# Mean and variance as sums on ScalarE, inputs rounded a pair of tiles ahead, and another order of the opening, in a block with fp4-rounded feed-forward layers

## The chip, the cores and the metric

The kernel runs on one core of one Trainium2 chip. The metric is the time of one execution on the device in microseconds (us); lower is better. Engines are named as the profile names them: PE is TensorE's matmul queue and PEld its weight loads, DVE is VectorE, ACT is ScalarE, POOL is GpSimd and SP is SyncE, which issues most transfers.

## The reference

The input x holds 2 x 2048 rows of D = 256 float32 numbers. Three parts follow each other, each with a layer norm in front and added back to x:

```python
x = x + 0.5 * ffn(layernorm(x))
x = x + attention(layernorm(x))
x = x + 0.5 * ffn(layernorm(x))

def layernorm(x):                       # over the 256 numbers of a row
    return (x - mean(x)) / sqrt(var(x) + 1e-5)

def fp4_quant_dequant(x):               # blocks of 16 along the last dimension
    scale = max(max(abs(block)) / 6, 1e-12)
    return round_to_grid(block / scale) * scale      # grid 0, .5, 1, 1.5, 2, 3, 4, 6, with sign

def fp4_linear(x, w):
    return fp4_quant_dequant(x) @ fp4_quant_dequant(w).T

def ffn(x):                             # w_gate, w_up: 704 x 256, w_down: 256 x 704
    return fp4_linear(silu(fp4_linear(x, w_gate)) * fp4_linear(x, w_up), w_down)
```

The attention has complex projections of 512 numbers from 256, a softmax over 2048 keys, and an output projection back to 256. Biases are added to all of its projections.

## The kernel before

**Tiles.** The 4096 rows make 32 tiles of 128 rows. Eight tiles share one SBUF array, xs[g], with g from 0 to 3. Everything stays in SBUF and all arithmetic is float32.

**Norm (L186 to L225).** One Norm object measures n tiles of a group. DVE does a bn_stats of each tile (L201), a bn_aggr of each (L204) and adds EPS (L206). ACT takes the square root (L209), which needs another function table than Silu (L442) or the exponential (L744); the switch is a row ACT_TABLE_LOAD. DVE refines the reciprocal with one Newton step (L212 to L221) and forms shift = -mean * rstd (L224). An Identity activation on ACT with both as pointers (L234) then writes the normalised tile.

**Rounding.** quant (L158 to L184) and the class Rounding (from L247 on, used in the opening) round to fp4: a reduction over blocks of 16 for the scale (L164), scale and reciprocal (L166, L168), a multiply (L170), an Abs on ACT (L179), two steps on DVE (L180, L182), and a last multiply by the scale (L184). For inputs and for pairs of h the last multiply runs on POOL.

**Feed-forward part.** inputs(i0) takes four tiles: the norm of the group if i0 is at its beginning, L234, the rounding of the 128 x 1024 array xl, and the transposes tx on PE (L403), whose results ACT copies to xqT (L404). products(i) computes gate and up of a tile on PE into gu (L428; PSUM has two buffers), with Silu on ACT (L442) and the multiply h = silu(gate) * up on DVE (L446). Two tiles of h are rounded together. turn(i) transposes h (th, L463) and copies it out on ACT (hqT, L464). back(i) multiplies by w_down (po, L472) and adds to x on DVE (L474). Tiles go through as units of two. At the first unit of every four tiles the whole of inputs for the next four is issued, ahead of the unit's products.

**Opening.** Up to about 90 us the weights are folded, rounded and transposed while tiles 0 to 11 are normalised and rounded and tiles 0 to 7 go through their products. These jobs are generators ("threads"), and the string ORDER names which one issues its next step: n0, n1 and n2 are norms of tiles 0 to 3, 4 to 7 and 8 to 15; g, u and d are halves of the weights; f folds the attention weights; x0 to x5 are inputs, two tiles each; p0 to p7 are products; h0 to h3 round pairs of h; t and b are turn and back. A fence ties every instruction to the one before it on its engine, so that the written order is the engines' order.

**Behind the opening** a scheduler orders each engine's instructions. Tiles 8 to 31 of the first feed-forward part run to about 300 us, the attention to about 840 us (scores ps at L708, the exponential at L744, products m at L805), and the second feed-forward part to the end. The norms of the attention and of the second feed-forward part are called early (measure in class Batch, and inputs), so that their instructions lie between others.

Of the kernel before, what the change touches and what calls it, by code (L numbers as in the profile page):

```python
# [10 lines left out]
FP = mybir.dt.float32  # L11
I32 = mybir.dt.int32
AF = mybir.ActivationFunctionType
ALU = mybir.AluOpType
# [3 lines left out]
P = 128  # L18
BLK = 16
EPS = 1e-5  # L20

# [4 lines left out]
BELOW = 1.0 - 2.0**-22  # L28
# [1 line left out]


ORDER = """
n0 n0 n0 g0 g0 g0 g0 n0 n0 g0 n0 g1 n0 g1 n0 f n0 g1 g0 n0 f g0 f n0 f g1 n0 g0 g1 x1 u1 x0 x1 u0 x0
f g1 f u0 g0 u1 g1 f x0 x1 g1 u0 x0 f n1 u1 g1 f f n1 u0 x0 n1 x0 x1 f n1 n1 u1 x1 n1 d1 u0 u1 x1 u0
n2 g1 n1 n2 n1 f u1 x0 d1 g1 n1 x0 x1 x0 n1 f u1 g0 x0 n1 x1 g0 p0 n1 x3 u1 u0 x2 p1 u1 n2 p0 d0 u1
x3 x1 u0 u0 x3 d0 d1 n2 d0 d1 d1 u1 p1 n2 x2 n2 u0 n2 x3 u0 x2 d0 x3 x1 n2 x3 x2 n2 p0 x3 x2 n2 d1
x2 d0 n2 p0 d0 n2 x3 n2 p1 p3 x2 p1 n2 x2 f n2 d0 h0 p3 d1 d0 h0 n2 p2 d1 p2 h0 x3 x4 x3 p3 x4 h0 x4
p3 p2 x2 p2 x4 x5 x5 h1 d0 x2 x5 p6 p4 x4 h0 h0 p6 p5 h1 x4 h0 p4 d1 x4 h0 x4 h1 p5 p4 p5 h1 h0 h1
x5 p4 d0 p5 p7 x4 h1 h2 d1 t0 p7 d1 x5 h1 x5 h2 t0 h1 p6 x5 p6 h2 h2 t1 p7 h1 h2 p7 h3 x4 d0 t1 x5
h2 b0 h3 t2 h3 x5 h3 t2 h2 b1 b0 t3 x5 h2 t3 h3 b1 h3 h3 b2 h2 h3 b3 b2 b3 h3  # L40
"""
TURNED = 4

# [9 lines left out]
def kernel(ctx: ExitStack, tc: tile.TileContext, x, wqT, bq, wkT, bk, wvT, bv, woT, bo,  # L53
                        w_gate, w_up, w_down, out):
    nc = tc.nc
    NB, S, D = x.shape
# [3 lines left out]
    GT = 8  # L60
# [76 lines left out]
    make_identity(nc, ident)  # L137
    ones = const.tile([P, P], FP, tag="ones", name="ones")
    nc.gpsimd.memset(ones, 1.0)
    tiny = const.tile([P, 1], FP, tag="tiny", name="tiny")  # L140
    nc.gpsimd.memset(tiny, 1e-12)

    wgu = const.tile([P, KD, 2 * FF], FP, tag="wgu", name="wgu")
    wd = const.tile([P, NR, D], FP, tag="wd", name="wd")
    nc.gpsimd.memset(wd[0:P - LAST, NR - 1, :], 0.0)
# [8 lines left out]
    def all_of(parts):  # L154
        for _ in parts:
            pass

    def quant(pool, y, n, tag, last, first=None):  # L158


        nb = n // BLK
        yb = y.rearrange("p (b k) -> p b k", k=BLK)
        scale = pool.tile([P, nb], FP, tag=f"{tag}_s", name=f"{tag}_s", bufs=2)
        nc.vector.tensor_reduce(scale, yb, AX.X, ALU.max, apply_absolute_value=True)  # L164
        yield
        nc.vector.scalar_tensor_tensor(scale, scale, 1.0 / 6.0, tiny.to_broadcast([P, nb]), ALU.mult, ALU.max)  # L166
        rec = pool.tile([P, nb], FP, tag=f"{tag}_r", name=f"{tag}_r", bufs=2)
        nc.vector.reciprocal(rec, scale)  # L168
        if first is None:
            nc.vector.scalar_tensor_tensor(  # L170
                yb, yb, BELOW, rec.unsqueeze(2).to_broadcast([P, nb, BLK]), ALU.mult, ALU.mult
            )
        else:
            nc.vector.scalar_tensor_tensor(rec, rec, BELOW, ones[:, 0:nb], ALU.mult, ALU.mult)
            first.tensor_tensor(yb, yb, rec.unsqueeze(2).to_broadcast([P, nb, BLK]), ALU.mult)
        yield

        m = pool.tile([P, n], FP, tag=f"{tag}_m", name=f"{tag}_m", bufs=2 if pool is wpool else 1)
        nc.scalar.activation(m, y, AF.Abs, scale=STEPS)  # L179
        nc.vector.scalar_tensor_tensor(y, m, LEAST, y, ALU.max, ALU.add)  # L180
        yield
        nc.vector.scalar_tensor_tensor(y, m, LEAST, y, ALU.max, ALU.subtract, reverse1=True)  # L182
        yield
        last.tensor_tensor(yb, yb, scale.unsqueeze(2).to_broadcast([P, nb, BLK]), ALU.mult)  # L184

    class Norm:  # L186

        def __init__(self, g, j0, n):  # L190
            self.g, self.j0, self.n = g, j0, n

        def turns(self, pool):
            g, j0, n = self.g, self.j0, self.n

            def tile(what, shape):
                return pool.tile(shape, FP, tag=what, name=f"{what}{g}_{j0}")

            mv, bn = tile("mv", [P, n, 2]), tile("bn", [P, n, 6])
            for j in range(n):  # L200
                nc.vector.bn_stats(bn[:, j, :], xs[g][:, j0 + j, :])  # L201
                yield
            for j in range(n):
                nc.vector.bn_aggr(mv[:, j, :], bn[:, j, :])  # L204
            var = tile("var", [P, n])
            nc.vector.tensor_scalar(var, mv[:, :, 1], EPS, None, ALU.add)  # L206
            yield
            sd = tile("sd", [P, n])
            nc.scalar.activation(sd, var, AF.Sqrt)  # L209
            yield  # L210
            self.rstd = rstd = tile("rstd", [P, n])
            nc.vector.reciprocal(rstd, sd)  # L212
            yield

            nc.vector.tensor_tensor(sd, rstd, rstd, ALU.mult)
            yield
            nc.vector.tensor_tensor(sd, sd, var, ALU.mult)
            yield
            nc.vector.tensor_scalar(sd, sd, -0.5, 1.5, ALU.mult, ALU.add)
            yield  # L220
            nc.vector.tensor_tensor(rstd, rstd, sd, ALU.mult)  # L221
            yield
            self.shift = tile("shift", [P, n])
            nc.vector.scalar_tensor_tensor(self.shift, mv[:, :, 0], -1.0, rstd, ALU.mult, ALU.mult)  # L224
            yield  # L225

    def normalise(pool, g, j0, n):
# [19 lines left out]
    class Rounding:  # L247
# [6 lines left out]
        def tile(self, what, n, bufs):  # L254
            return self.pool.tile([P, n], FP, tag=f"{self.tag}_{what}", name=f"{self.tag}_{what}", bufs=bufs)

        def turns(self, y, n):
            nb = n // BLK
            yb = y.rearrange("p (b k) -> p b k", k=BLK)

            def by_block(t):
                return t.unsqueeze(2).to_broadcast([P, nb, BLK])

            scale = self.tile("s", nb, self.bufs)
            nc.vector.tensor_reduce(scale, yb, AX.X, ALU.max, apply_absolute_value=True)
            yield
            nc.vector.scalar_tensor_tensor(scale, scale, 1.0 / 6.0, tiny.to_broadcast([P, nb]), ALU.mult, ALU.max)
            yield
            rec = self.tile("r", nb, self.bufs)
            nc.vector.reciprocal(rec, scale)  # L270
            yield
            if self.first:
                nc.vector.tensor_scalar(rec, rec, BELOW, None, ALU.mult)
                yield
                nc.gpsimd.tensor_tensor(yb, yb, by_block(rec), ALU.mult)
            else:
                nc.vector.scalar_tensor_tensor(yb, yb, BELOW, by_block(rec), ALU.mult, ALU.mult)
            yield
            m = self.tile("m", n, self.bufs_m)
            nc.scalar.activation(m, y, AF.Abs, scale=STEPS)  # L280
            yield

            nc.vector.scalar_tensor_tensor(y, m, LEAST, y, ALU.max, ALU.add)  # L283
            yield
            nc.vector.scalar_tensor_tensor(y, m, LEAST, y, ALU.max, ALU.subtract, reverse1=True)  # L285
            yield
            (nc.gpsimd if self.last else nc.vector).tensor_tensor(yb, yb, by_block(scale), ALU.mult)
            yield
# [100 lines left out]
    def ffn(phase, store, pools):  # L389
# [19 lines left out]
        def inputs(i0):  # L409

            g, j0 = divmod(i0, GT)
            if j0 == 0:
                stats[g] = normalise(small, g, 0, GT)
            yield
            xl = xp.tile([P, XT, D], FP, tag="xl", name=f"xl{phase}_{i0}")
            for u in range(XT):
                normed(xl[:, u, :], g, j0 + u, stats[g])
            yield
            yield from quant(xp, xl.rearrange("p u d -> p (u d)"), XT * D, "qx", nc.gpsimd)
            yield  # L420
            across(i0, xl, 0, XT)

        def product(which, i):
# [55 lines left out]
            yield  # L479

        xqTs, hs, hqTs = {}, {}, {}
        pending, turned = [], []
        first = 0
        if phase == 0:
            first, pending, stats[1] = opening(across, products, held, turn, back)
# [6 lines left out]

        units = [(i0, HT) for i0 in range(first, NT - HT, HT)] + [(i0, 1) for i0 in range(NT - HT, NT)]
        for i0, n in units:
            if i0 % XT == 0 and i0 + XT < NT and i0 + XT not in xqTs:
                all_of(inputs(i0 + XT))
            h = held(i0, n)
            for u in range(n):
                all_of(products(i0 + u))
                if turned:  # L500
                    all_of(back(turned.pop()))
                if len(pending) > HT:
                    all_of(turn(pending[0]))
                    turned.append(pending.pop(0))
                yield
            all_of(quant(later["pool"], h, n * FF, "qh", nc.gpsimd if n == HT else nc.vector))
            pending += range(i0, i0 + n)
# [8 lines left out]
    def opening(across, products, held, turn, back):  # L516
# [1 line left out]

        begun = len(nc.cur_bb.bb.instructions)
        hp = ffn0_pools[1]["pool"]  # L520
        norms = {"n0": Norm(0, 0, 4), "n1": Norm(0, 4, 4), "n2": Norm(1, 0, 8)}

        def inputs(k):

# [476 lines left out]
```

## Time and profile before

| | |
|---|---|
| median of 3 runs | 1074.61 us (1074.57 to 1074.98) |
| the profiled execution's own time | 1073.74 us |
| span of its profile, first to last instruction | 1071.9 us |
| PE busy | 1044.7 us (97%) |
| DVE busy | 805.8 us (75%), 1387 instructions |
| ACT busy | 469.9 us (44%), 739 instructions |
| POOL busy | 253.6 us (24%), 148 instructions |
| table loads on ACT (square root, L209) | 12 rows, 1283 ns each |

The profiled execution lies 0.87 us below the median and has 1.8 us outside its span. A group of instructions in the profile has its line, engine, operation and tile, then its count, its busy time, the mean of one in ns, and the idle time of the engine before it with what ended most of it. A wait has the waiting engine and line, the line waited for, and then the total in us, the number of times and the longest. Lines are those of the kernel before.

### The profile page before, as it was taken

To read this page: it belongs to the slowest core of one execution; us is meant where nothing else is said; L and a number is where in the kernel's file an instruction comes from. 1 tells how busy PE (TensorE), PEld (TensorE's weight loads), DVE (VectorE), ACT (ScalarE), POOL (GpSimd) and SP (SyncE) were. 2 spreads that over 40 slices of the span, in tenths; PEclk is the share of its full clock that TensorE was granted. 3 is DMA by queue.
4 is the path that set the end of the run, shared out by engine and by line. 5 is a ranking of instruction groups with operands and counts; after the bars stand their busy time and mean duration, and the time that the engine had idled before them with its cause. 6 is when DMAs were issued, how large, how long until landed. Compare 5 with 4: busy or idle time off the path is not lost.

```text
span 1071.9 us, 11329 instructions
## 1 busy us (share of the span) xinstructions
PE 1044.7 (97%) x4206; PEld 731.6 (68%) x4206; DVE 805.8 (75%) x1387; ACT 469.9 (44%) x739; POOL 253.6 (24%) x148
## 2 busy tenths in 40 slices
PE   6998999999999999999999999999999999999998
PEld 5676777777775666676675666666655777777776
DVE  7999998867634888576688958678767587777575
ACT  4754654544335735447343633343333244343232
POOL 4563121210103020111124111212461021221110
PEclk9999999999999999999999999999999999999999
DMA  9000000000000000000000000000000000000001
GB/s 321 1 1 1 1 1 1 1 1 1 0 1 1 1 1 0 1 1 1 0 1 1 1 0 1 1 1 1 0 1 1 10 20 10 20 10 20 20 10 40
DMA packets 7286, 13.50 MB, mean 13 GB/s; under 512 B 1344, under 2 KB 3648, under 8 KB 6848
## 3 DMA queue, kind: packets, MB, share of 16 engines
q1 hardware_dynamic: 6128, 12.13, 3.1%
q10 hardware_dynamic: 1104, 0.66, 0.3%
q8 instruction: 33, 0.54, 0.2%
q14 instruction: 21, 0.17, 0.1%
HBM read 8.59 MB, written 4.19 MB: 12 GB/s over the span
## 4 chain that ended last, share of the span: by engine, by line
PE 89%; DVE 7%; ACT 2%; DMA 1%; issue 1%; POOL 0%; SPq 0%; DVEq 0%; ACTq 0%; POOLq 0%
PE gu L428 26%; PE ps L708 19%; PE m L805 15%; PE po L472 14%; PE th L463 4%; PE poa L856 3%; PE pu L686 2%; PE z L783 2%; PE tx L403 1%; DVE st L743 1%; PE wm L338 1%; PE txa L624 1%; ACT xn L234 1%; DVE h L285 1%; DVE h L283 1%
## 5 line engine op out<-in xcount | busy, mean ns | idle before, releaser
L428 PE MATMUL gu<-wgu,xqT 128*128 128x352 f32 x1024 | 317.9, 460 | 3.0 <-DVE h L446 2.7
L428 PEld LDWEIGHTS gu<-wgu,xqT 128*128 128x128 f32 x1024 | 188.4, 190 | 97.6 <-DVE h L446 3.8
L708 PE MATMUL ps<-uT,xT 128*128 128x512 f32 x512 | 232.2, 593 | 0.7 <-DVE most L720 0.7
L472 PE MATMUL po<-wd,hqT 128*128 128x256 f32 x768 | 176.1, 379 | 0.0
L472 PEld LDWEIGHTS po<-wd,hqT 128*128 128x128 f32 x768 | 144.7, 190 | 28.2 <-ACT zT L819 0.6
L708 PEld LDWEIGHTS ps<-uT,xT 128*128 128x128 f32 x512 | 95.1, 190 | 93.2 <-issue 81.0
L720 DVE TENSOR_TENSOR most<-ps,most 128x512 f32<-128x512 f32 x112 | 77.0, 688 | 93.5 <-ACT st L715 92.8
L184 POOL TENSOR_TENSOR h<-h,qh_s 128x1408 f32<-128x1408 f32 x26 | 67.5, 2595 | 294.0 <-DVE h L182 252.1
L715 ACT COPY st<-ps 128x512 f32<-128x512 f32 x128 | 74.5, 583 | 134.1 <-PE ps L708 133.5
L805 PE MATMUL m<-tw,xn 128*128 128x256 f32 x448 | 124.9, 380 | 0.0
L464 ACT COPY hqT<-th 128x512 f32<-128x512 f32 (+1 forms) x128 | 55.4, 481 | 156.7 <-PE th L463 154.5
L772 POOL TENSOR_TENSOR sums<-tw,sums 128x512 f32<-128x512 f32 x42 | 56.9, 1354 | 232.3 <-DVE tw L768 212.9
L744 ACT ACTIVATE st<-st 128x1024 f32<-128x1024 f32 x64 | 67.5, 1057 | 76.0 <-DVE st L743 75.6
L805 PE MATMUL m<-st,xn 128*128 128x256 f32 x336 | 100.0, 379 | 0.0
L446 DVE TENSOR_TENSOR h<-h,gu 128x704 f32<-128x704 f32 x64 | 56.3, 879 | 55.5 <-PE gu L428 52.8
L805 PEld LDWEIGHTS m<-tw,xn 128*128 128x128 f32 x448 | 84.8, 190 | 13.1 <-DVE tw L767 1.2
L743 DVE TENSOR_TENSOR st<-st,top 128x1024 f32<-128x1024 f32 x64 | 83.2, 1312 | 0.8 <-ACT top L739 0.8
L805 PEld LDWEIGHTS m<-st,xn 128*128 128x128 f32 x336 | 63.2, 190 | 26.2 <-issue 19.4
L180 DVE SCALAR_TENSOR_TENSOR h<-qh_m,h 128x1408 f32<-128x1408 f32 (+1 forms) x30 | 45.8, 1527 | 33.1 <-ACT qh_m L179 32.9
L442 ACT ACTIVATE h<-gu 128x704 f32<-128x704 f32 x64 | 48.2, 753 | 44.9 <-PE gu L428 44.6
L179 ACT ACTIVATE qh_m<-h 128x1408 f32<-128x1408 f32 (+1 forms) x30 | 38.9, 1297 | 45.9 <-DVE h L170 42.1
L463 PE MATMUL th<-ident,h 128*128 128x128 f32 x384 | 53.1, 273 | 1.4 <-ACT hqT L464 1.4
(175 smaller groups left out, 1262.5 us busy)
## 6 DMA issues: line engine op xcount, KB each, us to landing
out_dram<-x SPq DMA_DIRECT2D x15, 256.0 KB, 2.1
x<-in_x_dram SPq DMA_DIRECT2D x3, 1024.0 KB, 13.1
n_down<-in_w_down_dram SPq DMA_DIRECT2D x1, 704.0 KB, 9.6
n_up<-in_w_up_dram SPq DMA_DIRECT2D x1, 640.0 KB, 6.2
x<-in_x_dram ACTq DMA_DIRECT2D x1, 512.0 KB, 5.4
wq_sb<-in_wqT_dram SPq DMA_DIRECT2D x1, 512.0 KB, 6.8
wk_sb<-in_wkT_dram SPq DMA_DIRECT2D x1, 512.0 KB, 4.5
wv_sb<-in_wvT_dram SPq DMA_DIRECT2D x1, 512.0 KB, 6.8
```

Of the source, the lines that this page charges most:

```text
L184: last.tensor_tensor(yb, yb, scale.unsqueeze(2).to_broadcast([P, nb, BLK]), ALU.mult)
L428: nc.tensor.matmul(out=ps[:, b2, 0:HALF], lhsT=xqT[:, i % XT, kc, :], rhs=wgu[:, kc, ts(which * 2 + b2, HALF)], start=(kc == 0), stop=(kc ...
L446: nc.vector.tensor_tensor(h, h, up, ALU.mult)
L463: nc.tensor.transpose(ps[:, r - r0, :], hq[:, chunk(r)], ident)
L472: nc.tensor.matmul(out=po, lhsT=hqT[:, r, :], rhs=wd[:, r, :], start=(r == 0), stop=(r == NR - 1))
L708: scored = nc.tensor.matmul(out=ps, lhsT=gr.of.xT[s][:, c, v, :], rhs=gr.uT[:, c, :], start=(c == 0), stop=(c == KD - 1),)
L715: nc.scalar.copy(piece[:, v, :], ps)
L720: seen = nc.vector.tensor_tensor(gr.most, ps, gr.most, ALU.max)
L743: nc.vector.tensor_tensor(piece, piece, gr.top.unsqueeze(1).to_broadcast([P, 2, Q]), ALU.subtract)
L744: nc.scalar.activation(piece, piece, AF.Exp, scale=SCALE)
L772: add(gr.sums, t[:, 1:3, :], gr.first[:, 1:3, :] if s == 1 else gr.sums, ALU.add)
L805: i = nc.tensor.matmul(out=gr.m[k], lhsT=left, rhs=right, start=first, stop=last)
```

## The change

1. Norm has a flag, summed, which is set for all norms but n0. With it ACT computes the sum of each tile as a Copy with an accumulator; DVE scales the sums by -1/D (least); ACT computes the sum of squared differences as a Square with least as its bias and an accumulator; DVE scales that and adds EPS. The activations' own outputs go to one scratch tile, each.
2. The constant tile tiny and its memset go. The scale is a tensor_scalar with an immediate in place of a scalar_tensor_tensor with a broadcast tile.
3. The last multiply of the input rounding runs on DVE for the four-tile inputs 12 and 16 of the first feed-forward part, and stays on POOL for the others.
4. Inputs of four tiles are begun one unit of two tiles earlier: the norm, L234 and the rounding are issued there, up to the mark "rounded", and the transposes stay at the unit where they were. Inputs 12 have no earlier unit and are issued as before.
5. ORDER has another sequence of steps.

In the instruction streams the matmul calls stay 2469. BNStats go from 96 to 4 and ACT's activations from 361 to 545; POOL's tensor_tensor from 137 to 135. On PE the transposes of tiles 12 to 15, tx_12, stand behind the gate product of tile 10 and half of its up product, where they stood ahead of both; from tile 12 on PE's order is nearly the old one. On DVE tile 8's L446 stands ahead of the L170 of tiles 12 to 15.

```diff
@@ -18,6 +18,7 @@
 P = 128
 BLK = 16
 EPS = 1e-5
+TINY = 1e-12
 
 
 
@@ -30,14 +31,15 @@
 
 
 ORDER = """
-n0 n0 n0 g0 g0 g0 g0 n0 n0 g0 n0 g1 n0 g1 n0 f n0 g1 g0 n0 f g0 f n0 f g1 n0 g0 g1 x1 u1 x0 x1 u0 x0
-f g1 f u0 g0 u1 g1 f x0 x1 g1 u0 x0 f n1 u1 g1 f f n1 u0 x0 n1 x0 x1 f n1 n1 u1 x1 n1 d1 u0 u1 x1 u0
-n2 g1 n1 n2 n1 f u1 x0 d1 g1 n1 x0 x1 x0 n1 f u1 g0 x0 n1 x1 g0 p0 n1 x3 u1 u0 x2 p1 u1 n2 p0 d0 u1
-x3 x1 u0 u0 x3 d0 d1 n2 d0 d1 d1 u1 p1 n2 x2 n2 u0 n2 x3 u0 x2 d0 x3 x1 n2 x3 x2 n2 p0 x3 x2 n2 d1
-x2 d0 n2 p0 d0 n2 x3 n2 p1 p3 x2 p1 n2 x2 f n2 d0 h0 p3 d1 d0 h0 n2 p2 d1 p2 h0 x3 x4 x3 p3 x4 h0 x4
-p3 p2 x2 p2 x4 x5 x5 h1 d0 x2 x5 p6 p4 x4 h0 h0 p6 p5 h1 x4 h0 p4 d1 x4 h0 x4 h1 p5 p4 p5 h1 h0 h1
-x5 p4 d0 p5 p7 x4 h1 h2 d1 t0 p7 d1 x5 h1 x5 h2 t0 h1 p6 x5 p6 h2 h2 t1 p7 h1 h2 p7 h3 x4 d0 t1 x5
-h2 b0 h3 t2 h3 x5 h3 t2 h2 b1 b0 t3 x5 h2 t3 h3 b1 h3 h3 b2 h2 h3 b3 b2 b3 h3
+n0 n0 n0 g0 g0 g0 g0 n0 g0 n0 g1 n0 n0 g1 n0 f n0 g0 f f g1 n0 g0 n0 g1 n0 f g0 u0 x1 g1 u0 u1 x0 f
+g1 g0 f f u0 x0 u0 f g1 u1 x0 u0 g0 n1 n1 x0 u1 u1 g0 n1 x0 x1 n1 x1 x0 n1 x1 x0 u1 f g1 u0 f x0 n1
+x1 n1 f n1 g1 n1 x1 x0 d0 u1 d0 n1 n1 n1 f x1 x0 g1 n2 n2 g1 n1 p1 x1 n1 u0 x1 n2 n1 p1 u1 n1 u0 n1
+u0 u1 x1 d1 x2 n2 d0 x2 u1 x3 d1 d1 p0 n2 d0 x2 p0 d0 x3 p2 d1 x2 n2 u0 p2 x3 x3 x3 u0 x2 d0 p3 x3
+x2 d1 u1 n2 d0 x3 x2 u1 d0 p3 p0 n2 d0 p1 n2 n2 n2 p0 d1 x2 n2 n2 x3 d1 p2 x3 n2 p1 n2 n2 h0 n2 h0
+n2 n2 h0 n2 h0 x2 p3 x3 x2 n2 h0 d1 n2 f h0 p3 p2 n2 h1 d0 n2 h0 n2 p5 p5 x5 h0 x4 d1 h0 h1 x5 p4 h1
+h1 d0 p4 d1 p4 x5 p5 x4 h1 x4 x5 h1 x4 p4 p5 d1 x4 x5 h1 x5 x5 t1 p6 x4 h1 p6 x5 p7 x4 p7 p6 h2 f h2
+t0 t1 h2 h2 h1 p7 t0 h2 b1 x4 p6 p7 h3 b1 h2 h3 t2 h3 t2 b0 x4 h3 x5 h2 b0 t3 t3 h3 h2 b2 x4 b2 h3
+b3 b3 h2 h3 h3 h3 x5
 """
 TURNED = 4
 
@@ -137,9 +139,8 @@
     make_identity(nc, ident)
     ones = const.tile([P, P], FP, tag="ones", name="ones")
     nc.gpsimd.memset(ones, 1.0)
-    tiny = const.tile([P, 1], FP, tag="tiny", name="tiny")
-    nc.gpsimd.memset(tiny, 1e-12)
-
+
+    each = const.tile([P, D], FP, tag="each", name="each")
     wgu = const.tile([P, KD, 2 * FF], FP, tag="wgu", name="wgu")
     wd = const.tile([P, NR, D], FP, tag="wd", name="wd")
     nc.gpsimd.memset(wd[0:P - LAST, NR - 1, :], 0.0)
@@ -163,7 +164,7 @@
         scale = pool.tile([P, nb], FP, tag=f"{tag}_s", name=f"{tag}_s", bufs=2)
         nc.vector.tensor_reduce(scale, yb, AX.X, ALU.max, apply_absolute_value=True)
         yield
-        nc.vector.scalar_tensor_tensor(scale, scale, 1.0 / 6.0, tiny.to_broadcast([P, nb]), ALU.mult, ALU.max)
+        nc.vector.tensor_scalar(scale, scale, 1.0 / 6.0, TINY, ALU.mult, ALU.max)
         rec = pool.tile([P, nb], FP, tag=f"{tag}_r", name=f"{tag}_r", bufs=2)
         nc.vector.reciprocal(rec, scale)
         if first is None:
@@ -171,7 +172,7 @@
                 yb, yb, BELOW, rec.unsqueeze(2).to_broadcast([P, nb, BLK]), ALU.mult, ALU.mult
             )
         else:
-            nc.vector.scalar_tensor_tensor(rec, rec, BELOW, ones[:, 0:nb], ALU.mult, ALU.mult)
+            nc.vector.tensor_scalar(rec, rec, BELOW, None, ALU.mult)
             first.tensor_tensor(yb, yb, rec.unsqueeze(2).to_broadcast([P, nb, BLK]), ALU.mult)
         yield
 
@@ -187,8 +188,8 @@
 
 
 
-        def __init__(self, g, j0, n):
-            self.g, self.j0, self.n = g, j0, n
+        def __init__(self, g, j0, n, summed=True):
+            self.g, self.j0, self.n, self.summed = g, j0, n, summed
 
         def turns(self, pool):
             g, j0, n = self.g, self.j0, self.n
@@ -196,14 +197,29 @@
             def tile(what, shape):
                 return pool.tile(shape, FP, tag=what, name=f"{what}{g}_{j0}")
 
-            mv, bn = tile("mv", [P, n, 2]), tile("bn", [P, n, 6])
-            for j in range(n):
-                nc.vector.bn_stats(bn[:, j, :], xs[g][:, j0 + j, :])
+            var, least = tile("var", [P, n]), tile("least", [P, n])
+            if self.summed:
+
+                for j in range(n):
+                    nc.scalar.activation(each, xs[g][:, j0 + j, :], AF.Copy, accum_out=var[:, j:j + 1])
+                    yield
+                nc.vector.tensor_scalar(least, var, -1.0 / D, None, ALU.mult)
                 yield
-            for j in range(n):
-                nc.vector.bn_aggr(mv[:, j, :], bn[:, j, :])
-            var = tile("var", [P, n])
-            nc.vector.tensor_scalar(var, mv[:, :, 1], EPS, None, ALU.add)
+                for j in range(n):
+                    nc.scalar.activation(
+                        each, xs[g][:, j0 + j, :], AF.Square, bias=least[:, j:j + 1], accum_out=var[:, j:j + 1]
+                    )
+                    yield
+                nc.vector.tensor_scalar(var, var, 1.0 / D, EPS, ALU.mult, ALU.add)
+            else:
+                mv, bn = tile("mv", [P, n, 2]), tile("bn", [P, n, 6])
+                for j in range(n):
+                    nc.vector.bn_stats(bn[:, j, :], xs[g][:, j0 + j, :])
+                    yield
+                for j in range(n):
+                    nc.vector.bn_aggr(mv[:, j, :], bn[:, j, :])
+                nc.vector.tensor_scalar(var, mv[:, :, 1], EPS, None, ALU.add)
+                nc.vector.tensor_scalar(least, mv[:, :, 0], -1.0, None, ALU.mult)
             yield
             sd = tile("sd", [P, n])
             nc.scalar.activation(sd, var, AF.Sqrt)
@@ -221,7 +237,7 @@
             nc.vector.tensor_tensor(rstd, rstd, sd, ALU.mult)
             yield
             self.shift = tile("shift", [P, n])
-            nc.vector.scalar_tensor_tensor(self.shift, mv[:, :, 0], -1.0, rstd, ALU.mult, ALU.mult)
+            nc.vector.tensor_tensor(self.shift, least, rstd, ALU.mult)
             yield
 
     def normalise(pool, g, j0, n):
@@ -264,7 +280,7 @@
             scale = self.tile("s", nb, self.bufs)
             nc.vector.tensor_reduce(scale, yb, AX.X, ALU.max, apply_absolute_value=True)
             yield
-            nc.vector.scalar_tensor_tensor(scale, scale, 1.0 / 6.0, tiny.to_broadcast([P, nb]), ALU.mult, ALU.max)
+            nc.vector.tensor_scalar(scale, scale, 1.0 / 6.0, TINY, ALU.mult, ALU.max)
             yield
             rec = self.tile("r", nb, self.bufs)
             nc.vector.reciprocal(rec, scale)
@@ -416,8 +432,10 @@
             for u in range(XT):
                 normed(xl[:, u, :], g, j0 + u, stats[g])
             yield
-            yield from quant(xp, xl.rearrange("p u d -> p (u d)"), XT * D, "qx", nc.gpsimd)
-            yield
+
+            last = nc.vector if phase == 0 and i0 <= 2 * GT else nc.gpsimd
+            yield from quant(xp, xl.rearrange("p u d -> p (u d)"), XT * D, "qx", last)
+            yield "rounded"
             across(i0, xl, 0, XT)
 
         def product(which, i):
@@ -479,7 +497,7 @@
             yield
 
         xqTs, hs, hqTs = {}, {}, {}
-        pending, turned = [], []
+        pending, turned, coming = [], [], {}
         first = 0
         if phase == 0:
             first, pending, stats[1] = opening(across, products, held, turn, back)
@@ -492,8 +510,13 @@
 
         units = [(i0, HT) for i0 in range(first, NT - HT, HT)] + [(i0, 1) for i0 in range(NT - HT, NT)]
         for i0, n in units:
+
             if i0 % XT == 0 and i0 + XT < NT and i0 + XT not in xqTs:
-                all_of(inputs(i0 + XT))
+                all_of(coming.pop(i0 + XT, None) or inputs(i0 + XT))
+            if i0 % XT == XT - HT and i0 + XT + HT < NT:
+                coming[i0 + XT + HT] = inputs(i0 + XT + HT)
+                while next(coming[i0 + XT + HT]) != "rounded":
+                    pass
             h = held(i0, n)
             for u in range(n):
                 all_of(products(i0 + u))
@@ -518,7 +541,7 @@
 
         begun = len(nc.cur_bb.bb.instructions)
         hp = ffn0_pools[1]["pool"]
-        norms = {"n0": Norm(0, 0, 4), "n1": Norm(0, 4, 4), "n2": Norm(1, 0, 8)}
+        norms = {"n0": Norm(0, 0, 4, False), "n1": Norm(0, 4, 4), "n2": Norm(1, 0, 8)}
 
         def inputs(k):
```

## The prediction

> **What bounds the kernel now.** I read busy time, the chain and the clock first, then what TensorE (PE) waited for, then windows of 20 us, last the groups that the change touches.
>
> ```profile
> PE 1044.7 (97%) x4206; PEld 731.6 (68%) x4206; DVE 805.8 (75%) x1387; ACT 469.9 (44%) x739; POOL 253.6 (24%) x148
> PEclk9999999999999999999999999999999999999999
> PE 89%; DVE 7%; ACT 2%; DMA 1%; issue 1%; POOL 0%; SPq 0%; DVEq 0%; ACTq 0%; POOLq 0%
> ```
>
> PE sets the end: 1044.7 of 1071.9 us, at a full clock. A change that leaves its 2469 matmul calls alone can win at most the 27.2 us in which PE stood. Its waits (us in total, times, longest) say where:
>
> ```profile
> PE we_q L330 <- DMA wq_sb<-in_wqT_dram: 8.1, 1, 8.1
> PE tx L403 <- POOL xl L184: 3.9, 2, 2.0
> PE gu L428 <- DVE h L446: 2.7, 2, 2.0
> PE pb L737 <- DVE mx L732: 2.3, 2, 1.6
> PE poa L856 <- DVE zT L830: 1.5, 1, 1.5
> PE we_k L330 <- ACT e_q L331: 1.4, 1, 1.4
> ```
>
> The first is the wait for the first weights, which stays. The second and third are stalls just behind the opening; the windows (PE, PEld, DVE, ACT, POOL busy, then clock, DMA share, GB/s) place them:
>
> ```profile
> 20.00:40.00 20.00, 19.24 (x102) 14.98 (x101) 19.97 (x64) 13.82 (x30) 11.57 (x7) 1.00 0.32 132
> 40.00:60.00 20.00, 20.00 (x75) 12.92 (x74) 19.57 (x37) 13.00 (x20) 11.31 (x8) 1.00 0.01 1
> 80.00:100.00 20.00, 17.66 (x74) 12.66 (x73) 18.77 (x21) 7.46 (x12) 9.05 (x3) 1.00 0.01 1
> 100.00:120.00 20.00, 17.96 (x85) 13.39 (x84) 18.77 (x53) 12.32 (x20) 4.53 (x2) 1.00 0.00 1
> 120.00:140.00 20.00, 18.15 (x83) 13.57 (x82) 17.85 (x36) 11.59 (x18) 4.52 (x2) 1.00 0.00 0
> ```
>
> From 80 to 140 us PE loses 2.34 + 2.04 + 1.85 = 6.2 us while VectorE (DVE) is 89 to 94% busy and ScalarE (ACT) 37 to 62%. From 20 to 60 us DVE is nearly full too, but PE loses only 0.8. The groups that the change touches:
>
> ```profile
> L201 DVE BATCH_NORM_STATS2 bn<-x 128x6 f32<-128x256 f32 x96 | 36.4, 409 | 6.1 <-DMA x<-in_x_dram 6.1
> L204 DVE BATCH_NORM_AGGREGATE mv<-bn 128x2 f32<-128x6 f32 x96 | 9.2, 150 | 0.0
> L234 ACT ACTIVATE xl<-x,shift,rstd 128x256 f32<-128x256 f32 x64 | 34.5, 596 | 1.0 <-DVE shift L224 1.0
> L184 POOL TENSOR_TENSOR xl<-xl,qx_s 128x1024 f32<-128x1024 f32 x13 | 26.2, 2013 | 74.7 <-DVE xl L182 60.5 <-ACT hqT L464 7.2 <-PE th L463 5.8
> L170 DVE SCALAR_TENSOR_TENSOR xl<-xl,qx_r 128x1024 f32<-128x1024 f32 x13 | 16.6, 1279 | 0.6
> L166 DVE SCALAR_TENSOR_TENSOR qx_s<-qx_s,tiny 128x64 f32<-128x64 f32 x13 | 7.6, 583 | 0.0
> ```
>
> **Sums on ScalarE.** 92 of 96 tiles lose a bn_stats and a bn_aggr. Started 0.33 and 0.07 us after one another, they hold DVE's queue 0.40 us a tile: 37 us, of it 9.6 us for the 24 tiles measured between 92 and 140 us. DVE gains one small op per norm (L206's like is 0.15 us): nothing.
>
> ACT gains a Copy and a Square per tile, each with an accumulator read. No row shows this at 256 elements. Nearest: L464's copy of 128x256, 0.38 us; L234, with two pointers, 0.60; L385, the one activation with an accumulator, 128x4, where a 0.19 us read starts 0.07 us behind its activation. Rows of one kind on ACT start about 0.1 us sooner than their length. Low end 0.8 us a tile (0.38 + 0.42, reads overlapped), high end 1.3 (0.50 + 0.60 + two reads of 0.1). I take 1.0, near 0.38 + 0.49 (one pointer, halfway) + 2 x 0.07. So 74 to 120 us more, 92 taken: ACT about 562 us, 52%.
>
> "ScalarE: Activation LUTs" (the Trainium skill, section Rules for kernel authors) speaks against such a move: simple adds and multiplies belong on VectorE. Here DVE is the full engine, so I let the windows overrule it. Its section What ACT_TABLE_LOAD costs gives 186 ns + 0.833 ns an element, 93 ns a pointer, 93 ns of overlap; an estimate by it is 0.31 + 0.40 = 0.71 us a tile without reads, and the sum would then sit nearer its fast rival.
>
> **Waits at tiles 8 to 16.** Before: L164 starts on DVE at 91.81 for tiles 12 to 15, with five bn_stats between it and tile 8's multiply L446, which comes only at 96.81 to 97.68; gu of tile 9 (up) has waited since 95.53 and starts at 97.73 (lost: 2.2). Then L182 ends at 100.27, POOL's L184 takes 100.42 to 102.35, and tx_12, PE in order behind it, starts at 102.41 (lost: 2.2).
>
> After: the order on DVE is reduce, scale, reciprocal, L446 of tile 8, L170, two rounding steps, L446 of tile 9, last multiply on DVE. From 91.8, with 1.1, 0.7, 0.4: L446 at 94.0 to 94.9, ahead of the 95.53 at which PE wants its buffer; that stall is gone. L170 to 96.1. ACT does Silu of tile 8 (to 91.76), eight Copies of 0.45 to 0.6 (to 95.4 or 96.6), the 1.06 us Abs (to 97.2 or 97.7), Silu 9. L180 and L182, 1.2 each, end at 99.6 to 100.1, L446 at 100.4 to 100.9, the multiply (1.3, from L170's row) at 101.7 to 102.2. By order PE now does gu_10_0 and half of gu_10_1 (3.55 us of matmuls) ahead of tx_12. From 95.53 that is 2.37 + 3.55 = 5.92, to 101.5. So tx_12 starts at 101.7 to 102.8, the latter with the hand-over and a slower Silu, against 102.41, but with 3.55 us more done. I take 102.7: saved 3.2 of 4.4.
>
> tx_16 lost 2.0 at 123.8 (POOL again, 123.83 to 125.76). Rounded a pair earlier and finished on DVE, its input is no longer last; but qx_m, Silu and hqT copies of 110 to 122 us now share ACT with 16 Copies and Squares and a table load of 1.28. I keep 1.1 of the 2.0: saved 0.9. The stall at 169 us (0.8; gu behind L446, which is queued behind L180 and L182) is halved by DVE's slack: 0.4.
>
> **Which queue pays.** With the last multiply on DVE, L446 and L164 of h queue behind 1.3 us instead of POOL's 2.0 plus hand-over; PE waits for L446. DVE has given up 9.6 us there and takes 2.6 back. The trace shows a hold between the two engines: at 81.67 L285 took 3.67 us instead of 1.62 while a POOL multiply took 3.90 instead of 2.59. POOL's h_6 multiply should be over before xl_12's, so the hold costs 0; if it meets it, up to 2.6. "SBUF — State Buffer" (the Trainium skill, Who interferes with whom) makes of this an exclusive lock for the whole instruction, which would favour taking xl off POOL.
>
> **tiny, immediates.** L166's 0.58 us includes holds; the shortest pointer form, 128x48, is 0.20, as is the tensor_scalar L273 of that shape. Zero.
>
> **New order of the opening.** PE is full from 40 to 80 us; its losses after the first matmul are 5.3 us before 20, 1.8 to 40, 0.3 to 60. The new order puts the first gate product ahead (about 29.6 instead of 30.9 us by the copies that must precede it) but postpones a 1.7 us row product and adds norm work to ACT. Zero, with -2 to +2.4 as ends (the latter below).
>
> **Pairs ahead elsewhere, attention, second FFN.** From 180 us on PE loses 8.2 us, none of it in waits for bn_stats; waits at 577 to 585 and 763 to 776 (pb, poa) have other causes and stay. Bursts of up to five Squares (2.5 us) now stand between score copies, where ACT is a third busy and scores have two buffers: 0, ends -1 and +1.5.
>
> **Sum.** -3.2 - 0.9 - 0.4 + 0 = -4.5. Profiled execution 1073.74 (span 1071.9 plus 1.8) becomes 1069.2; it lies 0.87 below the median of 1074.61, so 1070.1 for the median.
>
> **Rivals.**
> A, all of it goes: the pair costs 0.8 us, both tx waits and both gu waits vanish (7.1), and the fuller opening order wins 2. 1074.6 - 9.1 = 1065.5. For: DVE near-full in every lossy window. Against: ACT at 60%+ beside it. 0.2.
>
> B, one wait for another: Silu, hqT and xqT copies stand behind Copies and Squares, in order, and PE takes back what DVE gave. Only the 3.55 us reordering counts, half undone by later copies: about -1, 1073.6. For: ACT's 12.3 and 11.6 of 20 us from 100 to 140 before 24 us more are added, spread to 160. 0.18.
>
> C, slower: ACT becomes the bound of the opening. From 20 to 60 us it has 6.2 + 7.0 = 13.2 us free and receives twelve tiles of sums. Above 1.1 us a tile they don't fit; at 1.3 ACT falls 2.4 us behind, and the xqT_4 copies, which stand behind eight Squares and a square root, stop the products of tiles 4 to 7. The same price slows 92 to 126 us, leaving 2 of the 4.5, and attention adds 1.5: +2.4 - 2 + 1.5 = +1.9, 1076.5. Without a gain at all behind tile 8: +3.9. 0.14.
>
> That the sums don't leave DVE can't be: the instruction stream has 4 bn_stats left.
>
> **How the numbers follow.** Forecast 0.48, A 0.2, B 0.18, C 0.14. About 0.2% (2.15 us) is what can be told from no change; forecast and A lie below it, B and a mild C within. Faster 0.68, same 0.18, slower 0.14. Range: low 1065.0, just past A; high 1075.5 takes in B and the milder part of C; about 2 in 10 lie outside.
>
> **What would show it.** Right: "tx <- POOL xl L184" gone from the waits for tiles 12 and 16, PE above 18.5 of 20 in the three windows, DVE near 770 us, ACT near 560, Copy and Square rows of 0.4 to 0.5. Wrong: a row over 0.6 us or a read over 0.15 that does not overlap; ACT above 18 of 20 between 20 and 60 us; new "gu <- ACT xqT" or "th <- ACT hqT" waits of a microsecond; score waits near the bursts.

## The result, and the profile after

The changed kernel takes 1076.89 us (median of 9 runs, 1076.54 to 1077.90) against 1074.41 for the kernel before (median of 9): 1.0024 times as long, 95% interval 1.0015 to 1.0033. It is slower by 2.5 us. The profiled execution took 1076.89 with a span of 1075.1, 3.2 us more than the span before.

Busy time and chain of the page after:

```profile
PE 1045.9 (97%) x4206; PEld 731.5 (68%) x4206; DVE 788.7 (73%) x1218; ACT 559.0 (52%) x1107; POOL 247.8 (23%) x145
PE 83%; DVE 11%; ACT 4%; issue 1%; DMA 1%; POOL 0%; SPq 0%; DVEq 0%; ACTq 0%
```

ACT gained 89 us and DVE lost only 17, where the removed rows were worth 44 and the prediction expected DVE near 770 us. PE's part of the chain fell by 6 points, and DVE's rose by 4. The waits of PE that are new or longer (us in total, times, longest):

```profile
PE gu L446 <- DVE h L464: 5.9, 3, 2.6
PE po L490 <- ACT hqT L482: 1.0, 1, 1.0
PE gu L446 <- ACT wgu L316: 0.9, 1, 0.9
PE wt L315 <- ACT wqbk L369: 0.6, 1, 0.6
```

(L464 is the multiply that was L446.) The waits of tx for POOL are gone, as forecast. But gu now waits 5.9 us for DVE, where it was 2.7. The windows (PE, PEld, DVE, ACT, POOL busy, clock, DMA share, GB/s) place it:

```profile
20.00:40.00 20.00, 19.19 (x94) 14.31 (x95) 19.16 (x39) 19.18 (x55) 8.23 (x5) 1.00 0.31 126
40.00:60.00 20.00, 17.13 (x70) 11.21 (x69) 19.46 (x29) 15.70 (x36) 10.50 (x7) 1.00 0.00 0
60.00:80.00 20.00, 18.68 (x76) 12.53 (x75) 19.93 (x24) 10.65 (x22) 8.94 (x5) 1.00 0.00 1
80.00:100.00 20.00, 19.67 (x94) 15.52 (x93) 18.83 (x20) 9.96 (x21) 11.71 (x6) 1.00 0.00 1
100.00:120.00 20.00, 16.73 (x71) 10.96 (x70) 18.46 (x25) 17.26 (x46) 2.39 (x1) 1.00 0.00 0
120.00:140.00 20.00, 19.04 (x90) 14.39 (x90) 18.98 (x22) 16.38 (x41) 2.60 (x1) 1.00 0.01 1
```

PE was full from 40 to 80 us before; now it loses 4.2 there, and tile 8's gate product starts at 93.95 instead of 88.43. I sum what each matmul started later than its shape's usual interval (below, "loss"): before 80 us 7.4 before and 13.0 after (+5.6), from 80 to 180 us 8.4 and 6.4 (-2.0), behind that 11.6 and 11.2 (-0.4). These give the 3.2 us of the spans. So the stage that was to gain gained less than half, and the opening, priced at zero, lost more than that.

Two places show what DVE did there. From the timeline of the changed kernel (start, length, engine, line, operation):

```profile
54.39 2.55 DVE L233 TENSOR_TENSOR sd<-sd,var 128x8 f32<-128x8 f32 x1
56.86 1.67 DVE L464 TENSOR_TENSOR h<-h,gu 128x704 f32<-128x704 f32 x2
53.62 3.30 POOL L291 TENSOR_TENSOR h<-h,qh_r 128x1408 f32<-128x1408 f32 x1 [2.25 <-DVE qh_r L289]
100.82 1.62 DVE L167 TENSOR_SCALAR qx_s<-qx_s 128x64 f32<-128x64 f32 x1
99.80 2.59 POOL L303 TENSOR_TENSOR h<-h,qh_s 128x1408 f32<-128x1408 f32 x1 [3.29 <-DVE h L301]
```

A multiply of 128x8, 0.16 us elsewhere, takes 2.55: it ends when POOL's multiply ends, at 56.9 us. The same line over the whole kernel, before and after (shortest, median and longest in ns, first and last start):

```profile
L217 DVE TENSOR_TENSOR sd<-sd,var x13: 96/158/168, 11.9 to 866.5; 128x8 f32<-128x8 f32 x11, 128x4 f32<-128x4 f32 x2
L233 DVE TENSOR_TENSOR sd<-sd,var x13: 101/161/2551, 11.7 to 878.1; 128x8 f32<-128x8 f32 x11, 128x4 f32<-128x4 f32 x2
```

The two L464 behind the held multiply, for which PE waits 1.9 us, start at its end. At 100.8 the scale of tiles 12 to 15 is held in the same way, ahead of tile 8's L464 (PE waits 2.6). I add up how much DVE's operations were longer than the lower quartile of the same operation and shape, where that is over 0.1 us, until DVE begins tiles 12 to 15 (the "hold"). It is a rough measure: another rule for the usual length moves it by up to 1 us.

| DVE until it begins tiles 12 to 15 | before | after |
|---|---|---|
| ends at | 91.8 us | 99.6 us |
| idle | 8.7 | 9.3 |
| hold | 7.6 | 19.2 |
| the rest, its work | 75.4 | 71.0 |

The sums on ACT took 4.4 us of work from DVE, and 11.6 us of hold came in. The hold sits in 8 operations before and in 16 after, and every one of them overlaps an operation of POOL. All 16 are tensor_scalar operations or have two tensor inputs; of the 23 reductions, reciprocals and bn operations that overlap POOL in that stretch none is held.

### The profile page after: what moved, and what is told of

The parts are those of the page before. It is cut to its first block, busy times and chain, and to the rows that moved or that the text cites. A ratio compares the mean times of both kernels' runs of the same rounds, so it can differ in the third digit from the quotient of the medians.

```text
span 1075.1 us, 11511 instructions
## 1 busy us (share of the span) xinstructions
PE 1045.9 (97%) x4206; PEld 731.5 (68%) x4206; DVE 788.7 (73%) x1218; ACT 559.0 (52%) x1107; POOL 247.8 (23%) x145
## 4 chain that ended last, share of the span: by engine, by line
PE 83%; DVE 11%; ACT 4%; issue 1%; DMA 1%; POOL 0%; SPq 0%; DVEq 0%; ACTq 0%
PE gu L446 23%; PE ps L731 18%; PE po L490 14%; PE m L828 14%; PE th L481 3%; PE poa L879 3%; PE pu L709 2%; PE z L806 2%; DVE st L766 1%; PE tx L419 1%; ACT each L209 1%; DVE h L301 1%; ACT xn L250 1%; PE txa L647 1%; DVE h L299 1%
## 5 line engine op out<-in xcount | busy, mean ns | idle before, releaser
L446 PE MATMUL gu<-wgu,xqT 128*128 128x352 f32 x1024 | 318.4, 460 | 7.1 <-DVE h L464 5.9
L446 PEld LDWEIGHTS gu<-wgu,xqT 128*128 128x128 f32 x1024 | 188.0, 190 | 102.6 <-DVE h L464 5.6
L464 DVE TENSOR_TENSOR h<-h,gu 128x704 f32<-128x704 f32 x64 | 56.0, 879 | 59.2 <-PE gu L446 56.7
L828 PEld LDWEIGHTS m<-st,xn 128*128 128x128 f32 x336 | 63.2, 190 | 26.2 <-issue 19.6
L460 ACT ACTIVATE h<-gu 128x704 f32<-128x704 f32 x64 | 48.0, 750 | 30.7 <-PE gu L446 30.6
```

The lines of the kernel that those rows point to most:

```text
L446: nc.tensor.matmul(out=ps[:, b2, 0:HALF], lhsT=xqT[:, i % XT, kc, :], rhs=wgu[:, kc, ts(which * 2 + b2, HALF)], start=(kc == 0), stop=(kc ...
L464: nc.vector.tensor_tensor(h, h, up, ALU.mult)
L828: i = nc.tensor.matmul(out=gr.m[k], lhsT=left, rhs=right, start=first, stop=last)
```

## The experiments

Times are set against runs of the kernel before that were taken beside them. Where bn_stats come back (open_bn, old_order, bn_behind, late_sums, early_g2), their arrays are allocated once, for space. "Loss" and "hold" are those of the profiled execution. Theory 1 blames ACT's time for the sums, theory 2 the new order with single held operations ahead of L464. Loss also holds time in which PE ran at half clock (last section): before 80 us some 5.9 us of old_order_sums and 3.5 of order_alone, from 80 to 180 us 1.6 to 1.8 of open_bn, old_order_sums, bn_behind, mults_first and tiny_back, 3.3 of late_sums and about 2 of order_alone. The others have none.

| kernel | us | against before (interval) | loss to 80 / 80 to 180 us | hold |
|---|---|---|---|---|
| changed | 1076.89 | +2.5 (1.0015 to 1.0033) | 13.0 / 6.4 | 19.2 |
| open_bn | 1081.25 | +6.9 (1.0050 to 1.0078) | 16.7 / 6.8 | 20.1 |
| old_order | 1072.80 | -1.6 (0.9979 to 0.9996) | 7.4 / 7.2 | 8.3 |
| old_order_sums | 1087.14 | +12.8 (1.0105 to 1.0132) | 20.3 / 8.2 | 9.4 |
| bn_behind | 1080.71 | +6.4 (1.0047 to 1.0072) | 13.0 / 9.4 | |
| mults_first | 1075.78 | +1.7 (1.0006 to 1.0024) | 12.2 / 7.0 | 19.4 |
| thin_sums | 1075.97 | +1.9 (1.0011 to 1.0029) | 11.6 / 6.4 | 19.6 |
| ahead_dve | 1074.35 | +0.3 (0.9995 to 1.0013) | 7.5 / 8.6 | 7.6 |
| late_sums | 1078.33 | +4.3 (1.0025 to 1.0050) | 8.0 / 13.1 | |
| order_alone | 1089.06 | +14.6 (1.0118 to 1.0146) | 16.9 / 12.8 | 18.9 |
| h_on_dve | 1074.17 | -0.3 (0.9989 to 1.0007) | 10.7 / 6.1 | 12.6 |
| tiny_back | 1076.91 | +2.4 (1.0014 to 1.0031) | 12.4 / 6.8 | 19.0 |
| early_g2 | 1069.87 | -4.6 (0.9940 to 0.9967) | 7.9 / 3.8 | 8.3 |

**The opening: order or sums?**

open_bn:
```diff
-        norms = {"n0": Norm(0, 0, 4, False), "n1": Norm(0, 4, 4), "n2": Norm(1, 0, 8)}
+        norms = {"n0": Norm(0, 0, 4, False), "n1": Norm(0, 4, 4, False), "n2": Norm(1, 0, 8, False)}
```
and ORDER without tokens 5 to 9 of n1 and 9 to 17 of n2.

> The changed kernel, but norms n1 and n2 of the opening (tiles 4 to 15) measure with bn_stats on DVE again, at the places of the Copies in the new order; the tokens of the Squares are left out of ORDER, the rest of it is the same. The sums behind the opening stay. Theory 1 (twelve tiles of sums at a measured 1.17 us each fill ACT from 20 to 50 us and everything else on ACT comes late): PE's losses before 80 us fall from 13.0 to about 8 us, time about 1072. Theory 2 (the new order itself is at fault: DVE operations with two SBUF inputs or in a tensor_scalar stand behind POOL multiplies ahead of the multiply L464 that PE needs): the waits of 2.1 us at 56 and 1.5 us at 69 stay, losses before 80 us stay above 11, time 1076 to 1077.

It was slower still: +6.9, with losses of 16.7 us to 80 us. In the new order the sums are worth 4.4 us. Theory 1, ACT's time as the main cause, is out. Theory 2's "above 11" holds, but not its time: it left out that DVE is full and gets 4 us of work back.

old_order: open_bn with the ORDER string of the kernel before.

> The changed kernel with the ORDER of the kernel before and bn_stats in the opening's norms; sums on ACT behind the opening, inputs a pair ahead, the last multiply on DVE and the immediates stay. Both theories: PE loses 7.4 us before 80 us, as before the change. Behind that it tells what the rest of the change is worth with an opening that is on time: by the prediction's walk 4.5 us, so about 1070; if the sums behind the opening put new waits in the place of the old (2.8 us at 101 and 1.1 us at 125 in the changed kernel), about 1.9 us, so 1072.5.

The opening is back (7.4, hold 8.3) and the kernel is faster than before, by 1.6 us. open_bn and old_order both have bn_stats in the opening and all the rest of the change, so the order is worth 8.4 us between them. Behind the opening the gain is the lower of the two forecasts; the timeline of ACT shows why:

```profile
91.92 0.42 ACT L205 ACTIVATE each<-x 128x256 f32<-128x256 f32 x1
92.24 0.19 ACT L205 ACTIVATION_READ_ACCUMULATOR each<-x 128x1 f32 x1
92.46 0.42 ACT L205 ACTIVATE each<-x 128x256 f32<-128x256 f32 x1
92.78 0.19 ACT L205 ACTIVATION_READ_ACCUMULATOR each<-x 128x1 f32 x1
92.88 0.74 ACT L461 ACTIVATE h<-gu 128x704 f32<-128x704 f32 x1
```

Tile 8's Silu, which started at 91.00 before, stands behind eight Copies that nobody needs yet; its multiply on DVE falls behind a rounding step, and gu waits 2.7 us.

old_order_sums: after's norms with the old ORDER and a token of n1 or n2 put behind each of the next 5 or 9 tokens.

> As the kernel with the old ORDER, but with the opening's norms n1 and n2 as sums on ACT: one Square's token is put behind each of the next five (n1) and nine (n2) other tokens after the norm's last Copy. Theory 1: the load does the harm in any order, losses before 80 us of 12 us or more, time 1076 or more. Theory 2: the old order takes the sums with less than 2 us of loss, time about 1072 to 1074.

+12.8 us, as theory 1 had it and theory 2 had not: the sums do great harm at these places, with a hold near the one before (9.4), so the hold is not the only way to lose time in the opening. DVE's idle time there rose from 8.7 to 24.3 us, and PE's half clock makes up some 7.5 us of the losses. My places were crude, so this shows that sums in the opening need an order made for them, and not what the best one costs.

thin_sums: `each[:, 0:w]` and `xs[g][:, j0 + j, 0:w]` with w = 16 for n1 and n2.

> The changed kernel with the opening's 24 sum activations (n1, n2) over 16 of the 256 columns; the other 240 are left out of these sums. All instructions, their order and their accumulator reads stay, but a pair should take about 0.2 us less each, 4.8 us in all. Theory 1 (ACT's time for the sums): losses before 80 us fall from 13.0 to below 9.5, time 1073 or less. Theory 2 (order and holds on DVE): they fall by no more than 1.5 us, 1075.5 to 1077.

Losses to 80 us fell by 1.4, as theory 2 had it; the time against before fell by 0.6, which the intervals do not tell from nothing. The edit takes 4.8 us from the some 14 us that these sums hold ACT (12 tiles of 1.17 us), so a part of the loss may be ACT's; how much all 14 us cost, this run does not show. That they are not the main cause rests on open_bn, which has no sums in the opening and loses more.

mults_first: in ORDER p3 and p2 (fourth tokens) go ahead of the 22nd n2, p4's fourth ahead of the third x4.

> The changed kernel with three tokens of ORDER moved: the multiplies h = silu(gate) * up of tiles 3 and 2 ahead of the norm n2's multiply sd * var, which a POOL multiply held for 2.55 us, and that of tile 4 ahead of the scale of input pair 4, held for 1.99 us. Theory 2 (DVE operations held by POOL in front of the multiplies that PE waits for): the waits at 56 (2.1) and 69 us (1.5) go, losses before 80 us fall from 13.0 to about 9.5, time 1073.4. Theory 1 (ACT is late): those waits only turn into others, the time stays within 1 us of 1076.9.

The two waits for L464 went, and others came: 1.1 and 0.7 us for a Silu at 64 and 73 us. Losses fell by 0.8 only; the hold stayed at 19.4. Theory 2, two misplaced multiplies, falls. The Silu that is late at 64 us stands on ACT behind the normalisation L249 (2.08 us), which had waited for shift from DVE: with DVE late as a whole, another operation became the late one.

That gave a third theory: the new order puts DVE's two-input operations beside POOL's multiplies throughout, and DVE, full in the opening, loses the time for good.

order_alone: the kernel before with the new ORDER, without the same tokens as in open_bn.

> The kernel before with nothing but the new ORDER (the tokens of the Squares left out, bn_stats everywhere). Theory 3 (the new order sets DVE's two-input operations beside POOL's multiplies, so that DVE, which is full in the opening, is held: 19.2 us of such excess durations on DVE before 99 us in the changed kernel, 7.6 in the kernel before): about 20 us of excess, PE's losses before 80 us near 16 (as with bn_stats in the opening: 16.7, of which the 4 us of bn_stats are a part), time 1081 to 1084. Rival (the loss comes from the sums, or from immediates in the scale): losses near 8, time near 1075.

Windows of this kernel, columns as above:

```profile
40.00:60.00 20.00, 18.09 (x77) 12.07 (x75) 19.80 (x42) 8.40 (x16) 10.09 (x7) 1.00 0.00 0
60.00:80.00 20.00, 18.32 (x64) 12.01 (x65) 19.63 (x26) 12.48 (x20) 8.29 (x7) 0.91 0.00 1
```

DVE is full, ACT at 42 to 62%, and the hold is 18.9 us with no sum in the kernel and no immediate in its scale. The losses to 80 us are 16.9, as theory 3 has it, though 3.5 us of them are half clock (the 0.91 above is one such stretch). The time was 5 us worse than its forecast, since waits behind the opening grew too (12.8, with 5.1 us for POOL's xl at 145 us). This is the cleanest comparison of all: up to tiles 12 to 15 the kernel before and order_alone give DVE the same 163 operations. Their first operation on those tiles, in the kernel before and in order_alone:

```profile
91.81 1.21 DVE L164 TENSOR_REDUCE qx_s<-xl 128x64 f32<-128x1024 f32 x1
103.47 1.21 DVE L164 TENSOR_REDUCE qx_s<-xl 128x64 f32<-128x1024 f32 x1
```

DVE comes 11.7 us later, and its hold is 11.3 us longer (18.9 instead of 7.6).

h_on_dve:
```diff
-"h0": (True, True), "h1": (True, True), "h2": (True, True), "h3": (True, True),
+"h0": (False, True), "h1": (False, True), "h2": (False, True), "h3": (False, True),
```
and ORDER without the fourth token of each h.

> The changed kernel with the first block multiply of the four pairs of h in the opening on DVE (one operation of 1.6 us) instead of POOL (2.6 us, behind a small DVE operation of 0.2). DVE gets 4 x 1.4 = 5.6 us of work. Theory 3: the excess falls from 19.2 to about 10, DVE is through with the opening 2 to 4 us sooner than at 99.6, time 1073.5 to 1075.5. Rival (DVE's work itself bounds the opening, holds or not): DVE's opening ends 5 us later, time 1080 or more.

The hold fell by 6.6, DVE's work rose by 5.3, its opening ended at 97.2 instead of 99.6, and the time fell by 2.8 us. The hold stayed above the forecast of about 10, but the end and the time lie in the forecast ranges. More work on the full engine made it faster, since more held time went with POOL's operations than work came in. The hold is thus a cause and not only a sign. A shorter chain of rounding steps for h, with no hand-over to POOL, may have helped: DVE's idle time fell by about 1 us, and no run takes the two apart.

tiny_back: the scale as scalar_tensor_tensor against the broadcast tile.

> The changed kernel with the scale as a scalar_tensor_tensor against a broadcast tile again, in place of the tensor_scalar with an immediate. In the changed kernel six of these small operations were held for 0.7 to 1.8 us. If the immediate form is what POOL holds, the excess falls by 4 us or more and the time to 1075 or less; by theory 3 (it is the order) nothing changes: 1076.4 to 1077.4.

No change that can be told (+2.4, hold 19.0): the immediates are worth nothing, as predicted, and the older form is held as much.

**Behind the opening: what does the rest of the change bring?**

bn_behind: `norm = Norm(g, j0, n, False)` in normalise.

> The changed kernel, new ORDER and sums in the opening, but with bn_stats on DVE for all norms behind the opening. Losses before 80 us stay at 13.0 by either theory. If the sums behind the opening were a gain, tile 8's multiply is late by the bn_stats again and the time rises by 2 to 3 us, to 1079; if they only replaced one wait by another, it stays within 1 us of 1076.9.

+6.4: the sums behind the opening gain 3.9 us in the changed kernel, more than the 2 to 3 forecast.

ahead_dve: the kernel before with `coming`, "rounded" and `last` of the diff, nothing else.

> The kernel before, with its ORDER, its bn_stats everywhere and its scale operations, and only two parts of the change: inputs of four tiles begun a pair ahead, and the last multiply of inputs 12 and 16 on DVE. If DVE's relief by the sums is what pays behind the opening, the wait for tile 8's multiply (2.2 us at 95) and a wait at tiles 12 to 16 stay, and the time is 1073 to 1075; if these two parts carry the gain, 1071 to 1072.5, as good as the kernel with old ORDER and sums (1072.8).

No difference from before. The waits for tile 8's multiply (2.0) and for the inputs of tile 16 (2.0, now for DVE's last multiply) stay; one for an hqT copy at 158 us (1.8) is new. Without DVE's relief these parts only move the wait.

late_sums: old_order with `normalise(small, g, 0, GT, phase == 1)`.

> The kernel with the old ORDER (bn_stats in the opening, inputs ahead, last multiply on DVE, immediates), but sums on ACT only in the attention and the second FFN; the two norms of tiles 16 to 31 in the first FFN are bn_stats again. In the kernel with old ORDER ACT was 14 to 19 of 20 us busy from 80 to 160 us, and hqT copies and a Silu came late behind Copies and Squares. If that is what took back half of the gain, the time falls below 1072.3; if DVE's relief is worth more than ACT's load there, it rises to 1073.5 or more.

+4.3, or 5.8 us slower than old_order: DVE's relief is worth more than ACT's load there, as the second branch had it. In its profiled execution 3.3 us are two stretches at half clock behind the waits; without them the loss from 80 to 180 us would be 9.8 against 7.2. Waits of 1.7, 2.4, 1.5 and 1.2 us stand at 98, 129, 161 and 163 us.

early_g2: old_order with a fourth thread in ORDER, n3 = Norm(2, 0, 8): 6 tokens behind p5's third, 3, 1, 3 and 2 behind the first t1, the second t1, the second t2 and the second t3, and 2 at the end. Of its edit (rest is the square root and the Newton step of n3):
```diff
-            if j0 == 0:
+            if phase == 0 and i0 == 2 * GT:
+                all_of(rest)
+            elif j0 == 0:
```

> The kernel with the old ORDER (1072.8), in which the eight Copies and eight Squares of tiles 16 to 23 now stand in the opening, between 62 and 91 us where ACT was half idle; their square root and Newton step stay behind it. If ACT's queue at tiles 8 to 16 is what took back part of the gain there (a Silu behind eight Copies, a wait of 2.9 us at 96, one of 1.8 at 123), two thirds of these 4.7 us go: 1069.5 to 1071. If the waits are DVE's and POOL's, no change: 1072 to 1073.5.

1069.87, 4.6 us faster than before (0.9940 to 0.9967), the best of all. Losses from 80 to 180 us fell from 7.2 to 3.8. It is as fast as I had forecast the change to be, but it is another kernel. What is left of PE's waits in that stretch:

```profile
PE gu L450 <- DVE h L468: 1.1, 1, 1.1
PE gu L450 <- ACT h L464: 1.1, 1, 1.1
```

## Why the prediction was wrong

**The step that failed: "New order of the opening".** I took zero with ends of -2 and +2.4, from PE's idle time and the first gate product (which came at 30.6 us, not 29.6). It cost 5.6 us of PE's time even with the sums' relief, and 8.4 us between two kernels without the sums there. What it raised is DVE's hold, from 7.6 to 19.2 us. I had the held operations before my eyes (3.67 us instead of 1.62) and weighed them at one place only. What had to be asked was what the new order does to a DVE that is 96 to 100% busy from 20 to 80 us: the hold went up by 11.6 us, DVE's work down by 4.4, and DVE ended the opening 7.8 us later; PE's slack covered only a part. order_alone and h_on_dve show it. The 3.2 us of the spans are this step less the gains of 2.0 us from 80 to 180 us, where I had forecast 4.5, and of 0.4 behind that.

"SBUF — State Buffer" (the Trainium skill, Who interferes with whom) says the engine that starts first keeps the shared port for its whole instruction; operations with two SBUF inputs and tensor_scalar are among those that want it. The traces agree: the multiply of two inputs took 2.55 us instead of 0.16 and ended with POOL's 3.30, and all 16 held operations are of these kinds.

**Waits at tiles 8 to 16.** Tile 8's wait was to vanish, with 3.2 of 4.4 us saved up to tx_12. Losses there became 2.77 + 0.39 + 0.20 + 0.55 = 3.9. Two causes: POOL's last multiply of h_6 met the scale L167 (1.62 us, where the walk had 0.7 and the shortest row of it has 0.16; I had said "the hold costs 0"), and DVE reached tiles 12 to 15 at 99.6 us, 5.6 us behind the start of tile 8's gate product (93.95), where it had been 3.4 us behind. The saving of 0.9 at tx_16 was right, and so was its reason, ACT's copies (1.1 left, now for an hqT copy), the stall at 169 us went whole (0.8, not 0.4).

**Sums on ACT.** 0.54 us from one Copy to the next and 0.63 from one Square to the next: 1.17 a tile, not 1.0, inside the range. The rows of the changed kernel:

```profile
L209 ACT ACTIVATE each<-x,least 128x256 f32<-128x256 f32 x92 | 46.6, 506 | 4.2 <-DVE least L206 2.4
L204 ACT ACTIVATE each<-x 128x256 f32<-128x256 f32 x92 | 38.3, 416 | 15.7 <-DVE x L887 9.5 <-DVE x L492 5.0
L204 ACT ACTIVATION_READ_ACCUMULATOR each<-x 128x1 f32 x92 | 17.5, 190 | 0.0
```

A read starts 0.1 us ahead of its activation's end, and the next activation waits for the read (old_order above: a Copy from 91.92 to 92.34, its read from 92.24 to 92.43, the next Copy at 92.46). The relief of DVE was right in kind: 4.4 us in the opening in the new order, 3.9 behind it.

**Rivals.** C came near in time (1076.5) with the wrong cause. Its condition was met (1.17 is above 1.1, ACT 19.2 of 20 us busy from 20 to 40), but without any of these sums on ACT the new order lost more (open_bn), so that C's time lay near is luck. By thin_sums ACT's load may be a part of the loss. B was right that ACT's queue puts new waits behind the opening; in old_order two thirds of the forecast gain are missing, and early_g2, which moves sixteen sums out of that queue, got them back. Immediates, attention and second FFN (-0.4 behind 180 us) were right at zero.

Still open is which pairs of steps make the hold, one by one. The one order tried that has the sums in the opening and little hold is old_order_sums, which left DVE idle instead; what a good one brings is not known.

## What to carry to other kernels

When an order written by hand changes, count for a full engine not only its work but the time that its operations are held by another engine; here a relief of 4 us was lost as 12 us of holds came with it. Moving work to an engine with idle time pays where that engine's queue is idle too: the same sixteen activations were worth some 3 us more up to 30 us earlier than ahead of a Silu. Waits that were taken away one by one came back under another name while the engine behind them stayed late (mults_first, ahead_dve); look at that engine's sum over the stage first.

## What the runs showed of the hardware

A wait of PE can have a second price. In late_sums PE waits 2.4 us until 129.5, and the granted clock (third column from the right) then drops:

```profile
128.00:130.00 2.00, 0.46 (x4) 0.49 (x5) 2.00 (x5) 1.66 (x2) 0.00 (x0) 1.00 0.00 0
130.00:132.00 2.00, 2.00 (x9) 1.50 (x8) 1.65 (x3) 1.56 (x3) 0.00 (x0) 0.52 0.00 0
132.00:134.00 2.00, 2.00 (x7) 1.67 (x6) 1.63 (x6) 2.00 (x4) 0.00 (x0) 0.63 0.00 0
134.00:136.00 2.00, 2.00 (x14) 1.78 (x13) 1.87 (x3) 0.90 (x3) 0.00 (x0) 1.00 0.00 0
```

The clock lost 0.48 x 2 + 0.37 x 2 = 1.7 us, which is half speed for about 3.4 us, and PE lost 1.7 us by it. Two waits of 1.5 and 1.2 us within 4 us were followed by another such stretch, at 164 us. It does not come each time: the changed kernel's wait of 2.6 us had none in its profiled execution, and of ahead_dve's 11 runs, six with a mean clock of 1.000 (one such stretch makes it 0.998) took 1073.82 to 1074.35 and five with 0.998 took 1075.01 to 1075.56, some 1.5 us more. Of the kernel before, 52 of the 63 runs beside the experiments had 0.998 and were 0.6 to 0.8 us slower in the median than the others; early_g2 had 1.000 in all of its five, so that much of its 4.6 us may be the clock. The changed kernel took 1076.5 to 1077.9 with either clock; why it shows no difference is open. "TensorE: Matmul & The Clock Gate" (the Trainium skill, What's actually happening) tells of half rate after an idle window of about 3.4 us; here 2.4 us of waiting were enough in some executions.
